# A state-space scan whose input is formed by TensorE from diagonals, in a two-layer block on one core

## The chip, the cores and the metric

The program runs on one core of a Trainium2 chip. The core has five engines that run beside each other and wait for one another through semaphores: TensorE (PE in the profile; its weight loads are listed apart as PEld), VectorE (DVE), ScalarE (ACT), GpSimd (POOL) and SyncE (SP), which here only issues DMAs. TensorE writes to PSUM, eight banks of 128 partitions by 512 fp32 values; the other tiles lie in SBUF. GpSimd reads and writes SBUF alone. The metric is the device time of one execution in microseconds (us), lower is better. Three runs of the kernel before took 4177.97, 4184.37 and 4188.32 us.

## The reference, cut to what matters

The input x has 8 sequences (batches) of 512 tokens with 256 channels, in fp32. A first layer adds a Mamba block and an FFN with weights and activations rounded to four bits; a second layer adds block-sparse attention and a two-layer local transformer. The change is nearly all in the first layer:

```
xn = layernorm(x)
x_in, z = split(xn @ W_in.T)              # 512 channels each
u = silu(causal_conv4(x_in) + conv_b)
d_raw, B, C = split(u @ W_xproj.T)        # 16, 16, 16 columns
delta = softplus(d_raw @ W_dt.T + b_dt);  A = -exp(A_log)
for each token t:                         # h: 512 channels x 16 states
    h = exp(delta[t] * A) * h + (delta[t] * u[t]) * B[t]
    y[t] = sum over states of h * C[t]
out = ((y + D_param * u) * silu(z)) @ W_out.T
x1 = x + out + fp4_ffn(xn)
```

fp4_ffn rounds xn, the hidden activations and its three weight matrices in blocks of 16 values. The second layer then works on x1.

## The kernel before, in words

The first stage (pools of `s0`, the kernel's lines 143 to 378) handles one batch after another. Channels lie on partitions, in NC = 4 chunks of 128, and the 512 tokens run along the free axis. Four generators make up a batch. `head(b)` loads x, normalises it, transposes it (xt), forms u with a matmul and four VectorE operations per chunk, forms delta, and du = delta * u on GpSimd (line 272); it writes B and C to HBM (`bc_d`, line 252). `ffn(b)` does the four-bit FFN. `scan(b)` (lines 322 to 369) runs over two halves of two chunks, and in each half over the NS = 16 states. For one chunk and one state, called a unit here (64 units per batch, 512 in all), it does:

```
act.activation(da, delta[:, c, :], AF.Exp, scale=a_neg[:, c, n : n + 1])   # L338, into PSUM
dve.tensor_tensor(hh, du[:, c, :], bc[:, 0, :], ALU.mult)                  # L340
dve.tensor_tensor_scan(hh, da, hh, 0.0, ALU.mult, ALU.add)                 # L341
pool.tensor_tensor(hh, hh, bc[:, 1, :], ALU.mult)                          # L342
pe.matmul(ys[i], ident, hh, start=(n == 0), stop=(n == NS - 1))            # L343
```

bc holds one row of B and one of C, spread over all partitions by a DMA (line 330, SP's queue). The sum over states is a matmul with the identity that accumulates in a PSUM bank. After a half, z = silu(...) is formed by channels (line 349), D_param * u is added on VectorE (line 355) and the gate multiplied on GpSimd (line 358). At the end `ps_o` (line 364) projects out and the sum goes to HBM as x1.

Before the first head, ten blocks of weights are rounded to four bits and transposed: eight for w_gate and w_up (lines 177 to 194) and two for w_down (lines 209 to 213). `beside` interleaves generators in program order: scan(b) with the chain of ffn(b) and head(b+1), 34 steps against 24. That order gives priorities; the planner of the tile framework simulates the program and writes each engine's instruction order by priority and by what is ready in its simulation. On the chip each engine then runs its list strictly in that order, and waits at the first instruction whose inputs are not there. A tile's `bufs` says how many buffers rotate under its tag: `da` has two PSUM banks, `mm` four, the two sums `y0` and `y1` one each; `h` has four SBUF buffers, `bc` three.

The second stage (pools of `s1`, from line 381) first loads its weights, builds two rotary tables on VectorE and writes them to HBM (lines 431 to 444), all on SP's queue, then loads x1 of batch 0 (line 390, called by `proj(0)`), and runs attention and the transformer over the batches. Its tiles may use the memory of the first stage only when the first stage's pools have been released.

## Time and profile before

| | |
|---|---|
| median of three runs | 4184.37 us |
| the profiled execution | 4182.33 us, of which the profile's span is 4180.5 us |
| granted TensorE clock, mean over the span | 0.883 |
| first stage: first scan instruction, last output matmul ends | 111.9 us, about 1808 us |
| second stage: first matmul of `ps_qk` | 1850.5 us |
| busy share of the span: PE, DVE, ACT, POOL | 83%, 69%, 41%, 35% |

The profile has one row per group of equal instructions, with total busy time, the mean duration of one, and the idle time of the engine ahead of them with what ended it. A matmul's duration includes some 0.17 us in which the result leaves the array while the next one already runs, so durations of matmuls overlap, and what a stream of them costs is read from the distance between starts. An fp32 matmul appears as two instructions of the same shape, each with its own weight load; a transpose of 128 x 128 appears as one.

### The profile page before, as it was taken

How to read it: one execution, taken by the hardware profiler on the slowest of the kernel's cores; microseconds unless marked ns; L12 is line 12 of the kernel's file. 1: busy time of each engine (PE TensorE's matmuls, PEld its weight loads, DVE VectorE, ACT ScalarE, POOL GpSimd, SP SyncE). 2: the span in 40 equal slices, each digit the busy share in tenths (PEclk: the TensorE clock that was granted, in tenths of full speed). 3: DMA queues.
4: the chain of work that ended last, by engine and by line, in shares of the span. 5: the costliest groups of instructions: out<-in, count | busy, mean ns of one | idle time of the engine just before them, and what ended most of it. 6: DMA issues, size and time to landing. Idle time of an engine off the chain costs nothing.

```text
span 4180.5 us, 40473 instructions
## 1 busy us (share of the span) xinstructions
PE 3488.5 (83%) x13932; PEld 1700.7 (41%) x13932; DVE 2892.1 (69%) x4825; ACT 1721.5 (41%) x3411; POOL 1456.9 (35%) x1059
## 2 busy tenths in 40 slices
PE   3677777777777777759999999999989999999998
PEld 1233333333333333324454544554554544445445
DVE  6899999999999999955545545654555455456454
ACT  2454545555454545414423333343243244234333
POOL 2666665657575757521111120111021011101211
PEclk9777787787887888879999999999999999999999
DMA  2333233333332323330111010010011101110100
GB/s 63 76 81 91 77 90 80 87 81 86 78 88 80 87 76 90 80 120 26 42 37 37 31 57 26 26 52 30 27 52 42 37 26 42 36 47 26 47 27 6
DMA packets 121606, 239.27 MB, mean 57 GB/s; under 512 B 10025, under 2 KB 41769, under 8 KB 121401
## 3 DMA queue, kind: packets, MB, share of 16 engines
q1 hardware_dynamic: 118464, 230.32, 19.7%
q10 hardware_dynamic: 2936, 6.36, 0.4%
q8 instruction: 111, 1.82, 0.2%
q14 instruction: 95, 0.77, 0.1%
HBM read 226.69 MB, written 9.96 MB: 57 GB/s over the span
## 4 chain that ended last, share of the span: by engine, by line
PE 46%; DVE 10%; issue 3%; ACT 2%; POOL 2%; DMA 1%; SPq 0%; POOLq 0%; DVEq 0%; ACTq 0%
PE ps_qkv L683 8%; PE ps_g L853 5%; PE ps_a L853 4%; PE ps_qk L514 3%; PE ps_wo L815 3%; PE ps_y L888 2%; PE ps_w L871 2%; PE ps_st L609 2%; PE lo L787 2%; PE ps_ls L735 2%; PE pt_qk L674 2%; DVE pr L764 2%; DVE nm L745 1%; PE pt L773 1%; DVE hh L341 1%
## 5 line engine op out<-in xcount | busy, mean ns | idle before, releaser
L343 PE MATMUL y<-hh,ident 128*128 128x512 f32 x1024 | 692.3, 789 | 407.5 <-POOL hh L342 406.1
L342 POOL TENSOR_TENSOR hh<-hh,bc 128x512 f32<-128x512 f32 x512 | 754.0, 1482 | 553.9 <-issue 130.3
L341 DVE TENSOR_TENSOR_SCAN hh<-da,hh 128x512 f32<-128x512 f32 x512 | 609.4, 1205 | 1.9 <-ACT da L338 1.2
L340 DVE TENSOR_TENSOR hh<-du,bc 128x512 f32<-128x512 f32 x512 | 575.6, 1145 | 32.8 <-PE y L343 23.8
L338 ACT ACTIVATE da<-delta,a_neg 128x512 f32<-128x512 f32 x512 | 349.3, 689 | 488.4 <-DVE hh L341 486.6
L343 PEld LDWEIGHTS y<-hh,ident 128*128 128x128 f32 x1024 | 204.1, 231 | 813.1 <-POOL hh L342 739.9
L702 POOL TENSOR_TENSOR r<-r,r 128x512 f32<-128x512 f32 x128 | 162.8, 1272 | 385.4 <-DVE r L700 385.4
L751 ACT ACTIVATE pr<-ps_ls,nm 128x256 f32<-128x256 f32 (+1 forms) x512 | 221.7, 446 | 176.7 <-DVE nm L745 176.6
L860 DVE SCALAR_TENSOR_TENSOR ht<-ps_a,b,gl 128x512 f32<-128x512 f32 x96 | 72.0, 750 | 264.1 <-PE ps_a L853 261.2
L463 POOL MEMSET sa<- 128x1 f32 x16 | 1.6, 98 | 725.4 <-DVE sa L819 386.2
L698 DVE TENSOR_TENSOR r<-ps_qkv,tab 128x512 f32<-128x512 f32 x128 | 87.9, 686 | 220.6 <-ACT sq L697 220.6
L853 PE MATMUL ps_g<-hn,wf 128*128 128x512 f32 (+1 forms) x384 | 212.1, 671 | 24.9 <-issue 24.3
L859 ACT ACTIVATE gl<-ps_g,b 128x512 f32<-128x512 f32 x96 | 65.9, 686 | 392.3 <-PE ps_g L853 392.3
L697 ACT ACTIVATE sq<-ps_qkv 128x512 f32<-128x512 f32 x128 | 76.6, 598 | 293.2 <-PE ps_qkv L683 293.2
L853 PE MATMUL ps_a<-hn,wf 128*128 128x512 f32 (+1 forms) x384 | 197.1, 634 | 0.0
L613 ACT ACTIVATE pt_e<-ps_st 128x512 f32<-128x512 f32 (+1 forms) x384 | 172.8, 536 | 15.2 <-PE ps_st L607 14.6
L745 DVE TENSOR_REDUCE nm<-ps_ls 128x2 f32<-128x512 f32 (+1 forms) x256 | 147.5, 618 | 44.7 <-PE ps_ls L735 43.8
L683 PE MATMUL ps_qkv<-wqkv,s 128*128 128x512 f32 x384 | 174.7, 604 | 0.0
L683 PE MATMUL ps_qkv<-wqkv,sf 128*128 128x512 f32 x384 | 173.4, 601 | 0.0
L764 DVE TENSOR_SCALAR pr<-pr,lrs 128x256 f32<-128x256 f32 (+1 forms) x512 | 148.7, 332 | 4.8
L338 ACT ACT_TABLE_LOAD x115 | 147.5, 1283 | 5.8 <-DVE hh L341 3.8
L735 PE MATMUL ps_ls<-lkt,lqt 64*128 64x256 f32 (+1 forms) x1024 | 140.0, 396 | 0.0
(212 smaller groups left out, 6450.8 us busy)
## 6 DMA issues: line engine op xcount, KB each, us to landing
bc<-bc_d SPq DMA_DIRECT2D x256, 512.0 KB, 4.9
wqkv<-in_wqkv SPq DMA_DIRECT2D x16, 1536.0 KB, 6.4
wf<-in_wf SPq DMA_DIRECT2D x16, 1364.0 KB, 5.9
wf<-in_wf SPq DMA_DIRECT2D x16, 768.0 KB, 4.8
tab<-tab SPq DMA_DIRECT2D x18, 512.0 KB, 4.3
wo<-in_wo SPq DMA_DIRECT2D x16, 512.0 KB, 3.9
x<-in_x SPq DMA_DIRECT2D x8, 512.0 KB, 5.4
x<-xs ACTq DMA_DIRECT2D x8, 512.0 KB, 5.8
```

Source lines behind the costliest of these rows:

```text
L338: act.activation(da, delta[:, c, :], AF.Exp, scale=a_neg[:, c, n : n + 1])
L340: dve.tensor_tensor(hh, du[:, c, :], bc[:, 0, :], ALU.mult)
L341: dve.tensor_tensor_scan(hh, da, hh, 0.0, ALU.mult, ALU.add)
L342: pool.tensor_tensor(hh, hh, bc[:, 1, :], ALU.mult)
L343: pe.matmul(ys[i], ident, hh, start=(n == 0), stop=(n == NS - 1))
L613: act.activation(pt[:, :n], banks[g][:, :n], AF.Exp)
L683: pe.matmul(ps, shifted(s, k, t * P, P), wqkv[:, k, i * IN : (i + 1) * IN], start=(k == 0), stop=(k == KC - 1),)
L735: pe.matmul(banks[r][:, i * nk : (i + 1) * nk], qt[LD * r : LD * (r + 1), 2 * p + i, w * P : (w + 1) * P], kt[LD * r : LD * (r + 1), 2 * p ...
L745: dve.tensor_reduce(nm, banks[r][:, : 2 * nk].rearrange("p (g n) -> p g n", g=2), AX.X, ALU.max, negate=True)
L751: act.activation(pr[:, at], banks[r][:, at], AF.Exp, bias=nm[:, i : i + 1], accum_out=rs[:, i : i + 1],)
L764: dve.tensor_scalar(pr[:, at], pr[:, at], rs[:, i : i + 1], None, ALU.mult)
L853: pe.matmul(dst[:m], wf1[:, k, off + c * P : off + c * P + m], hn[:, k, :], start=(k == 0), stop=(k == KC - 1),)
```

## The change

The change has five parts. (1) The product of du and B is taken from VectorE. `head` transposes du to tokens (`dut`) and B to tokens (`bt`). For each state, VectorE builds once per batch four diagonal matrices of B (`dg`, 128 x 512), and for each unit TensorE forms bu = dut^T x diag(B) with four fp32 matmuls of 128 columns, in PSUM (three banks, tag `bu`). The scan reads bu from PSUM, and the decay `da` now lies in SBUF. (2) The sum over states is done by `add`: four transposes of 128 x 128 that accumulate in PSUM, so that y comes out by tokens. D_param * u is scaled on ScalarE and enters the same sum. (3) The gate z is formed by tokens, multiplied on VectorE with y, transposed back on TensorE (`ps_zt`, `zt`) and projected out. (4) The rounding of the FFN's weights becomes a generator that runs beside scan(0), and the rotary tables are made behind it, with fewer and larger VectorE operations. (5) Buffers: `mm` has three banks for four; the spread DMA carries C alone; `xn`, `xd`, `xq` and `xs` lose buffers or go; the ffn yields more often; the second stage's pools may take memory tile by tile (`reuse_waits="tile"`), x1 of batch 0 is loaded first there, and the first `fetch` comes after `proj(0)`.

```diff
-        pmm = s0.enter_context(tc.tile_pool(name="pmm0", bufs=4, space=PSUM))
-        pda = s0.enter_context(tc.tile_pool(name="pda0", bufs=2, space=PSUM))
+        pmm = s0.enter_context(tc.tile_pool(name="pmm0", bufs=3, space=PSUM))
+        pbu = s0.enter_context(tc.tile_pool(name="pbu0", bufs=3, space=PSUM))
...
-        for name, dst in (("w_gate", w_g), ("w_up", w_u)):
...
-        for r in range(D // P):
...
+        def fp4_weights():
+            for name, dst in (("w_gate", w_g), ("w_up", w_u)):
+                src = a[name].rearrange("(j p) d -> p j d", p=FB)
+                for j in range(0, FI // FB, 2):
+                    raw = q.tile([P, FI], FP, tag="q_src", name="q_src")[:FB, : 2 * D]
+                    act.dma_start(raw.rearrange("p (j d) -> p j d", j=2), src[:, j : j + 2, :])
+                    fp4(raw, raw, FB, 2 * D, q, sm)
...
+                    yield
...
+        tab_d = [dram.tile([P, 4, NT, LD], FP, tag=f"tab_{l}", bufs=1, name=f"tab_{l}") for l in range(DEPTH)]
+
+        def rotary_tables():
+
+            for l in range(DEPTH):
+                tab = one.tile([P, NT, DI], FP, tag="z", name="tab")[:, :2, :].rearrange("p (i t) (u d) -> p (i t u) d", t=1, d=LD)
+                tab = tab.rearrange("p (i t) d -> p i t d", t=NT)
+                sp.dma_start(tab, a["rotary"])
+                for i, name in ((0, "q_scale"), (2, "k_scale")):
+                    qs = sm.tile([P, LD], FP, tag="qs", bufs=2, name="qs")
+                    sp.dma_start(qs, a[name][l].unsqueeze(0).to_broadcast([P, LD]))
+                    if i == 0:
+                        dve.tensor_scalar(qs, qs, 8.0, None, ALU.mult)
...
+                    for at, cols, sc in ((i, lo, lo), (i, hi, hi), (i + 1, lo, hi), (i + 1, hi, lo)):
+                        dve.tensor_tensor(tab[:, at, :, cols], tab[:, at, :, cols], by(sc), ALU.mult)
+                sp.dma_start(tab_d[l], tab)
+                yield
...
-            xn = w1.tile([P, NT, D], FP, tag="xn", name="xn")
+            xn = one.tile([P, NT, D], FP, tag="xn", name="xn")
...
-            xd = w1.tile([DR + 2 * NS, L], FP, tag="xd", name="xd")
+            xd = w1.tile([DR + 2 * NS, L], FP, tag="xd", bufs=1, name="xd")
             act.copy(xd, ps[: DR + 2 * NS, :])
-            bc_d = dram.tile([2 * NS, L], FP, tag="bc_d", name="bc_d")
-            sp.dma_start(bc_d, xd[DR:, :])
+            c_d = dram.tile([NS, L], FP, tag="c_d", name="c_d")
+            sp.dma_start(c_d, xd[DR + NS :, :])
+
+            nx = DR + 2 * NS
+            ps = pmm.tile([P, L], FP, tag="mm", name="ps_bt")
+            for t in range(NT):
+                pe.transpose(ps[:, t * nx : (t + 1) * nx], xd[:, t * P : (t + 1) * P], ident[:nx, :nx])
+            bt = w1.tile([P, NT, NS], FP, tag="bt", name="bt")
...
-            du = w1.tile([P, NC, L], FP, tag="du", name="du")
+            dut = w1.tile([P, NT, DI], FP, tag="dut", name="dut")
...
-                pool.tensor_tensor(du[:, c, :], delta[:, c, :], u[:, c, :], ALU.mult)
-                yield
-            made[b] = x, xn, xt, u, bc_d, delta, du
+
+                pool.tensor_tensor(e, delta[:, c, :], u[:, c, :], ALU.mult)
+                yield
+                ps = pmm.tile([P, L], FP, tag="mm", name="ps_du")
+                for t in range(NT):
+                    pe.transpose(ps[:, t * P : (t + 1) * P], e[:, t * P : (t + 1) * P], ident)
+                evac(dut[:, :, c * P : (c + 1) * P], ps.rearrange("p (t d) -> p t d", d=P))
+            yield
+            made[b] = x, xn, xt, u, c_d, bt, delta, dut
...
+                    yield
...
-                ys = [py.tile([P, L], FP, tag=f"y{i}", name=f"y{i}") for i in range(2)]
+                ys = [py.tile([P, NT, P], FP, tag=f"y{i}", name=f"y{i}") for i in range(2)]
+
+                def add(y, src, first, last):
+
+                    for t in range(NT):
+                        pe.matmul(
+                            y[:, t, :], src[:, t * P : (t + 1) * P], ident, is_transpose=True,
+                            start=(first and t == 0), stop=(last and t == NT - 1), skip_group_check=True,
+                        )
+
+                for i in range(2):
+                    c = c0 + i
+                    ud = rot.tile([P, L], FP, tag="h", bufs=5, name="ud")
+                    act.activation(ud, u[:, c, :], AF.Copy, scale=d_par[:, c : c + 1])
+                    add(ys[i], ud, True, False)
                 for n in range(NS):
-                    bc = rot.tile([P, 2, L], FP, tag="bc", name="bc")
-                    sp.dma_start(
-                        bc,
-                        bc_d.rearrange("(t n) l -> n t l", n=NS)[n].unsqueeze(0).to_broadcast([P, 2, L]),
-                    )
+                    cb = rot.tile([P, L], FP, tag="cb", name="cb")
+                    sp.dma_start(cb, c_d[n].unsqueeze(0).to_broadcast([P, L]))
+                    if c0 == 0:
+                        dg[n] = one.tile([P, NT, P], FP, tag=f"dg{n}", name=f"dg{n}")
+                        dve.tensor_tensor(
+                            dg[n], ident.unsqueeze(1).to_broadcast([P, NT, P]),
+                            bt[:, :, n : n + 1].to_broadcast([P, NT, P]), ALU.mult,
+                        )
                     for i in range(2):
                         c = c0 + i
-
-                        da = pda.tile([P, L], FP, tag="da", name="da")
+                        bu = pbu.tile([P, L], FP, tag="bu", name="bu")
+                        for t in range(NT):
+                            pe.matmul(
+                                bu[:, t * P : (t + 1) * P], dut[:, t, c * P : (c + 1) * P], dg[n][:, t, :],
+                                start=True, stop=True,
+                            )
+                        da = rot.tile([P, L], FP, tag="da", name="da")
                         act.activation(da, delta[:, c, :], AF.Exp, scale=a_neg[:, c, n : n + 1])
-                        hh = rot.tile([P, L], FP, tag="h", bufs=4, name="hh")
-                        dve.tensor_tensor(hh, du[:, c, :], bc[:, 0, :], ALU.mult)
-                        dve.tensor_tensor_scan(hh, da, hh, 0.0, ALU.mult, ALU.add)
-                        pool.tensor_tensor(hh, hh, bc[:, 1, :], ALU.mult)
-                        pe.matmul(ys[i], ident, hh, start=(n == 0), stop=(n == NS - 1))
+                        hh = rot.tile([P, L], FP, tag="h", bufs=5, name="hh")
+                        dve.tensor_tensor_scan(hh, da, bu, 0.0, ALU.mult, ALU.add)
+                        pool.tensor_tensor(hh, hh, cb, ALU.mult)
+                        add(ys[i], hh, False, n == NS - 1)
                     yield
-                for i in range(2):
-                    c = c0 + i
+                for t in range(NT if c0 == 0 else 0):
                     ps = pmm.tile([P, L], FP, tag="mm", name="ps_z")
                     for k in range(KC):
                         pe.matmul(
-                            ps, w_in[:, k, DI + c * P : DI + (c + 1) * P], xt[:, k, :],
+                            ps, xt[:, k, t * P : (t + 1) * P], w_in[:, k, DI:],
                             start=(k == 0), stop=(k == KC - 1),
                         )
-                    z = rot.tile([P, L], FP, tag="t1", name="z")
-                    act.activation(z, ps, AF.Silu)
-                    dve.scalar_tensor_tensor(
-                        u[:, c, :], u[:, c, :], d_par[:, c : c + 1], ys[i], ALU.mult, ALU.add
-                    )
-                    pool.tensor_tensor(u[:, c, :], u[:, c, :], z, ALU.mult)
-                yield
-            xs = sums.pop(b)
...
+                    act.activation(z[:, t, :], ps, AF.Silu)
+                for i in range(2):
+                    zc = z[:, :, (c0 + i) * P : (c0 + i + 1) * P]
+                    dve.tensor_tensor(zc, zc, ys[i], ALU.mult)
+                yield
             for t in range(NT):
+                ps = pmm.tile([P, L], FP, tag="mm", name="ps_zt")
+                for c in range(NC):
+                    pe.transpose(ps[:, c * P : (c + 1) * P], z[:, t, c * P : (c + 1) * P], ident)
+                zt = rot.tile([P, NC, P], FP, tag="zt", bufs=1, name="zt")
+                evac(zt, ps.rearrange("p (c n) -> p c n", n=P))
                 ps = pmm.tile([P, L], FP, tag="mm", name="ps_o")
                 for c in range(NC):
-                    pe.matmul(
-                        ps[:, :D], u[:, c, t * P : (t + 1) * P], w_o[:, c, :],
-                        start=(c == 0), stop=(c == NC - 1),
-                    )
-                dve.tensor_tensor(xs[:, t, :], xs[:, t, :], ps[:, :D], ALU.add)
-            act.dma_start(x1_d[b], xs)
-
-        sums = {}
+                    pe.matmul(ps[:, :D], zt[:, c, :], w_o[:, c, :], start=(c == 0), stop=(c == NC - 1))
+                dve.tensor_tensor(x[:, t, :], x[:, t, :], ps[:, :D], ALU.add)
+            act.dma_start(x1_d[b], x)
...
-            beside(scan(b), chain(*rest), 34, 24)
+            if b == 0:
+                rest = [fp4_weights(), *rest, rotary_tables()]
+            beside(scan(b), chain(*rest), 34, 37 if b else 49)
...
-        w0 = s1.enter_context(tc.tile_pool(name="w1", bufs=1))
...
+        w0 = s1.enter_context(tc.tile_pool(name="w1", bufs=1, reuse_waits="tile"))
...
+        x1_first = load_x1(0)
...
-            x1 = x1s[b] = load_x1(b)
+            x1 = x1s[b] = load_x1(b) if b else x1_first
...
-        fetch(0, 0, "wqkv", "tab", "wo", "wf1", "wf2")
         tc.keep_in_program_order(act.preload_act_table_set("natural_log_exp_and_others"))
         alone(proj(0))
+        fetch(0, 0, "wqkv", "tab", "wo", "wf1", "wf2")
```

## The prediction

> **What bounds the kernel now.** I read the page first, then its groups, then busy time by stretches, then who waited for whom, and last the order of time around short matmuls.
>
> The page says PE 83% and DVE 69%, but these are means over two stages:
>
> ```profile
> PE   3677777777777777759999999999989999999998
> DVE  6899999999999999955545545654555455456454
> PEclk9777787787887888879999999999999999999999
> ```
>
> After the first slice of 104.5 us come sixteen with VectorE at 80 to 90% or more and TensorE at 60 to 70% on a clock of 0.7 to 0.8; then they change places. The change lies in the first stage, so VectorE's rows count there:
>
> ```profile
> L343 PE MATMUL y<-hh,ident 128*128 128x512 f32 x1024 | 692.3, 789 | 407.5 <-POOL hh L342 406.1
> L342 POOL TENSOR_TENSOR hh<-hh,bc 128x512 f32<-128x512 f32 x512 | 754.0, 1482 | 553.9 <-issue 130.3
> L341 DVE TENSOR_TENSOR_SCAN hh<-da,hh 128x512 f32<-128x512 f32 x512 | 609.4, 1205 | 1.9 <-ACT da L338 1.2
> L340 DVE TENSOR_TENSOR hh<-du,bc 128x512 f32<-128x512 f32 x512 | 575.6, 1145 | 32.8 <-PE y L343 23.8
> L338 ACT ACTIVATE da<-delta,a_neg 128x512 f32<-128x512 f32 x512 | 349.3, 689 | 488.4 <-DVE hh L341 486.6
> ```
>
> The scan waits for nobody (1.9 us of idle time in 512), ACT waits for the scan, TensorE waits for GpSimd. By stretches (us, busy PE, PEld, DVE, ACT, POOL with counts, then the granted clock, the DMA share, GB/s):
>
> ```profile
> 400.00:1600.00 1200.00, 895.79 (x2010) 392.61 (x2010) 1112.72 (x1310) 630.63 (x820) 749.72 (x512) 0.79 0.33 83
> 1757.00:1803.00 46.00, 32.20 (x68) 11.21 (x67) 41.09 (x40) 18.01 (x23) 27.61 (x21) 0.96 0.38 90
> 1803.00:1850.50 47.50, 6.14 (x25) 4.36 (x25) 15.04 (x85) 1.92 (x4) 6.22 (x14) 0.61 0.68 226
> ```
>
> VectorE is busy 92.7% of the steady stretch: it is the bound. The third line is the passage between the stages, 47.5 us with every engine idle most of the time. TensorE's waits in the same 1200 us:
>
> ```profile
> PEld y L343 <- POOL hh L342: 506.8, 223, 5.7
> PE y L343 <- POOL hh L342: 275.5, 161, 4.1
> ```
>
> In order of time, the first scan instruction starts at 111.9 us, later batches follow every 210.5 and then 215.0 us, the eighth begins at 1612.6 and ends at 1803.9. One batch therefore holds 0.927 x 215 = 199 us of VectorE, and by the same division 134 us of GpSimd and 113 us of ACT.
>
> **Short matmuls.** The change replaces 512-column matmuls by 128-column ones, so their price decides. Durations include the tail; I take start to next start in the second stage, where the clock is full:
>
> ```profile
> 2057.23 0.82 PE L674 MATMUL pt_qk<-ident,r 128*128 128x128 f32 x6
> 2057.89 0.38 PE L728 MATMUL ps_ls<-mask,identb 128*128 128x256 bf16 x2
> 2058.20 0.72 PE L735 MATMUL ps_ls<-lkt,lqt 64*128 64x128 f32 x8
> 2058.84 0.87 PE L78 MATMUL ps_tr<-ident,xn 128*128 128x128 f32 x6
> 2064.63 1.88 PE L514 MATMUL ps_qk<-s,wq 128*128 128x512 f32 x4
> 2066.35 0.60 PE L728 MATMUL ps_ls<-mask,identb 128*128 128x512 bf16 x2
> ```
>
> Six transposes take 2057.89 - 2057.23 = 0.66 us, 0.11 each. Four 512-column fp32 instructions take 1.72 us, 0.43 each, 0.84 ns per column. L735 is nearest to the new matmul: 128 columns with a weight load of 128 columns before each, in two halves of the rows side by side; a half does four in 0.64 us, first load included, so 0.16 each, and 0.11 if only the columns counted.
>
> **The cost, per unit (one chunk, one state; 64 per batch).**
> - VectorE loses L340: 72.0 us per batch. It gains 16 `dg` products per batch; the nearest row is L340 itself, whose instructions last 0.62 us undisturbed and 1.145 in the mean, so 9.9 to 18.3 us; I take 18. It gains two evacuations each of `dut` and `zt` (the copies of 128x512 in these rows last 0.69): 2.8. The gate product replaces L355 (0.75), nothing. VectorE: 199 - 72 + 18 + 3 = 148 us.
> - TensorE. Before, at full clock, per batch, columns at 0.84 ns: y 128 x 0.43 = 55; `ps_in` and `ps_z` 32 x 0.43 = 14; `ps_xp` and `ps_dt` 16 x 0.43 = 7; `ps_g`, `ps_u` 64 x 0.295 = 19; `ps_d`, `ps_o` 80 x 0.215 = 17; 40 transposes 4.4. That is 116 us in a batch of 215. After: y goes; `add` is four transposes, 0.44 per unit, 28 us; bu is eight instructions. Low end 0.11, the columns alone; high end 0.11 + 0.19 (the weight load's own duration) = 0.30. L735 shows the load hidden after the first, so 0.115: 0.92 per unit, 59 us. 48 further transposes (ud, `dut`, `zt`): 5. Sum 116 - 55 + 28 + 59 + 5 = 153 us.
> - GpSimd loses L358 (four of 1.27) and some of the disturbance by L340 (L342 has 1.26 undisturbed, 1.48 mean): 134 falls to 115 to 129. ACT gains four ud copies (0.69), half of the evacuations (0.6 each) and `bt`: 113 to 118; writing `da` to SBUF instead of PSUM is unseen here; its row is 0.69, the SBUF-to-SBUF exponential of `head` 0.62, so I take no change, and 5 us per batch of either sign.
> - DMA: half the bytes of bc. Only 4.8 us of waits on it are in the whole run; nothing.
>
> So the bound moves to TensorE: 153 us at full clock against 148 on VectorE. Two terms stretch it. The clock: 0.79 now, in gaps; 0.96 in the stretch 1757 to 1803, with TensorE only 70% busy but evenly so, and 0.95 over the second stage. With little idle time left I take 0.95: 161 us. Waits: `add` still waits for GpSimd in order, and bu of later units queues behind it on TensorE's list, and the scans behind bu. Now these waits are 275.5 / 1200 x 215 = 49 us per batch. Three banks of bu (3.6 us of scans) stand between, so I take half, 25 us. A batch: 186 us, against 215. A check: with columns at 0.84 ns and row or column groups side by side, the second stage's rows sum to about 1790 us of its 2330, 0.77; 153 / 186 is 0.82.
>
> **The Trainium skill against this.** "TensorE: Matmul & The Clock Gate", Part 4, says that a transpose costs about 275 ns in a kernel and does not count as activity for the clock. The durations here agree (0.27), the pitch of 0.11 does not, and the clock holds through the transposes above. By the page's figure `add` would be 64 x 4 x 0.275 = 70 us instead of 28, the batch about 230 and the total about 4215 us. I go by the pitch.
>
> **Moved work.** The ten weight blocks leave the front. x lands at 13.9 us; its normalisation takes 6; from the first transpose of xn (71.3) to the first scan (111.9) are 40.6; with the new transposes and the first dg and bu I put the first scan at 63, 49 us earlier. Their cover is scan(0), where they cost VectorE ten passes of 3.0 to 3.8 us and copies, 36 us, and the tables 5: 148 + 41 = 189, at 92.7% busy 204. Ten loads move onto ACT's queue beside the exponentials, and eight table DMAs onto SP's, where cb of scan(1) queues behind a table that waits for z's buffer; a few us each, so 210 for batch 0: no change. If batch 0's cover fails, at most those 41 us come back.
> Between the stages, x1 is loaded at 1840.2 behind the tables' round trips; weights arrive from 1808. Without them x1 comes with the weights, and the first `ps_qk` starts about 20 us after the scan's end instead of 46.6: 27 us, between 12 (only the last table's wait) and 45 (memory freed early). What is late next is the weights' own load, 5 us. The deferred fetch has 45 us until its first use.
>
> **Sum** on the profiled execution (4182.3, 2 us under the median): front -49, batch 0 0, six batches 6 x -29 = -174, last batch 191 to 166 (no head beside it) -25, passage -27: -275. 4182 - 275 = 3907 us.
>
> **Rivals.**
> - *Engines overlap better.* No lasting waits for GpSimd; VectorE binds at 148 / 0.927 = 160 and TensorE at 161, batch 165. Seven times 21 less: 3760 us. For it: even supply in a scan-only stretch. Against: two engines this full with three banks between.
> - *TensorE waits as now.* The whole 49 us stay: 161 + 49 = 210; seven times 24 more: 4075 us. For it: GpSimd's long rounding products (1.7 us) and 4 us waits. At a clock of 0.79 it would be the same with 16 us of waits.
> - *Slower: bu's weight loads are not hidden.* At 0.30 per instruction bu is 154 us, TensorE 248, a batch 286, seven and three quarter times 100 more, about 4680 us. It decides from the point where 275 us are eaten: 275 x 0.95 over 7.6 x 512 instructions is 0.067 us more, a pitch of 0.18. L735 speaks against it, but with half the rows each.
> - *It does little:* gain and stalls cancel, a batch near 222, about 4182.
>
> **How the numbers follow.** My case 0.42 (3830 to 3990), better overlap 0.20, waits as now 0.20, slower 0.15, no change 0.03. A run of this kernel tells 0.3%, 12 us, from no change. Faster 0.82, same 0.03, slower 0.15. The range runs from 3750, the better overlap, to 4190; it leaves out the slower case and the tail below.
>
> **What the next profile would show.** If right: in the scan's steady stretch TensorE above 90% busy at a clock above 0.9, VectorE near 80%; the scan row idle for PE's bu; bu's starts 0.11 to 0.12 apart; first scan near 63 us; `ps_qk` near 1575. Wrong if bu's starts lie 0.18 or more apart, if the clock stays at 0.8, or if `add` waits 40 us or more per batch for GpSimd.

## The result

The changed kernel takes 4304.52 us (median of four runs, 4297.69 to 4305.67), the kernel before 4181.17 beside it (four runs, 4168.83 to 4188.32): a ratio of 1.0305, 95% interval 1.0279 to 1.0331. It is slower by 3%, where a gain of 6.6% was forecast, and above the upper end of the range, 4190. The profiled execution of the changed kernel took 4297.69 us, its span 4295.9.

Time by stages, from the starts of the first scan instruction of each batch in both traces. A "steady batch" is here and below the mean of batches 1 to 6; the last batch is counted to the start of its last scan instruction.

| stage | before, us | after, us | difference | forecast |
|---|---|---|---|---|
| start to first scan | 111.9 | 56.8 | -55 | -49 |
| batch 0 | 210.5 | 283.8 | +73 | 0 |
| a steady batch (six) | 215.0 | 233.7 | +18.7 (+112) | -29 (-174) |
| last batch | 186.4 | 209.2 | +23 | -25 |
| last scan to first `ps_qk` | 51.5 | 24.7 | -27 | -27 |
| from `ps_qk` to the end | 2330 | 2319 | -11 | 0 |

What was moved out of the front and the passage came out as forecast. Everything that has a scan in it went the other way.

The page of the changed kernel, busy tenths in 40 slices:

```profile
PE   5587877787877778778999999999999999999998
DVE  5766666657575766655564455555545655555454
PEclk7898989898999989898999999999999999999999
```

VectorE fell from 8 and 9 tenths to 5 to 7 in the scan's slices, as it should, but TensorE did not take its place: 7 and 8 tenths. No engine is full any more. The same over the six steady batches (us, then busy PE, PEld, DVE, ACT, POOL with counts, the granted clock, the DMA share, GB/s):

```profile
340.60:1742.70 1402.10, 1093.35 (x6310) 830.04 (x6311) 914.79 (x1163) 682.69 (x905) 709.35 (x528) 0.93 0.14 43
```

A batch holds 915 / 6 = 152 us of VectorE, where 148 were forecast, and 1093 / 6 = 182 us of busy TensorE at a clock of 0.93, where 161 (153 at full clock, stretched by 0.95) were. The groups of the page that answer to those of before:

```profile
L405 POOL TENSOR_TENSOR hh<-hh,cb 128x512 f32<-128x512 f32 x512 | 690.6, 1355 | 798.3 <-DVE hh L404 712.0
L404 DVE TENSOR_TENSOR_SCAN hh<-da,bu 128x512 f32<-128x512 f32 x512 | 613.7, 1211 | 275.1 <-PE bu L397 250.5
L374 PE MATMUL y<-ident,hh 128*128 128x128 f32 x2048 | 354.3, 299 | 325.7 <-POOL hh L405 322.3
L397 PE MATMUL bu<-dg,dut 128*128 128x128 f32 x4096 | 577.8, 289 | 5.4 <-DVE hh L404 5.3
```

The scan, which waited 1.9 us before, now waits 250.5 us for bu in the whole run; bu itself waits for almost nothing, but the `add` (L374) that stands between two bu on TensorE's list waits 322.3 us for GpSimd. Who waits for whom in the six steady batches (us, times, longest):

```profile
DVE hh L404 <- PE bu L397: 183.1, 155, 3.7
PE y L374 <- POOL hh L405: 239.8, 273, 3.6
DVE h L346 <- PE ps_u L341: 76.1, 36, 3.0
...
PE ps_du L310 <- POOL e L306: 47.7, 24, 4.4
```

The last two lines are of the other work: the feed-forward's product on VectorE waits for TensorE, and the new transposes `ps_du` wait for GpSimd's `e`. They turned out to be the ones to follow. The price of the short matmuls is not the cause, as a stretch of the timeline shows (start, us, engine, line, operation, count):

```profile
1252.33 1.28 PE L397 MATMUL bu<-dg,dut 128*128 128x128 f32 x10
1253.54 0.45 PE L283 MATMUL ps_bt<-ident,xd 48*128 48x48 f32 x4
...
1260.46 0.66 PE L374 MATMUL y<-ident,hh 128*128 128x128 f32 x4 [1.29 <-POOL hh L405]
1260.95 0.61 PE L397 MATMUL bu<-dg,dut 128*128 128x128 f32 x4
```

Ten bu in 1253.54 - 1252.33 = 1.21 us, 0.12 each; over all of them the median from start to start is 0.112, the forecast's 0.115. The last two lines show the order: bu starts when the `add` ahead of it has waited its 1.29 us for GpSimd.

### The profile page after: what moved, and what is told of

Read it like the earlier page. It is cut to its first block, busy times and chain, and to the rows that moved or that the text cites. A ratio compares the mean times of both kernels' runs of the same rounds, so it can differ in the third digit from the quotient of the medians.

```text
span 4295.9 us, 51035 instructions
## 1 busy us (share of the span) xinstructions
PE 3660.6 (85%) x19452; PEld 2249.7 (52%) x19468; DVE 2503.9 (58%) x4441; ACT 1727.3 (40%) x3446; POOL 1321.0 (31%) x1027
## 4 chain that ended last, share of the span: by engine, by line
PE 56%; DVE 19%; POOL 12%; issue 8%; ACT 3%; DMA 1%; DVEq 0%; POOLq 0%; ACTq 0%; SPq 0%
PE ps_qkv L732 7%; POOL hh L405 7%; DVE hh L404 6%; PE ps_g L902 4%; PE ps_a L902 4%; PE bu L397 3%; PE y L374 3%; PE ps_qk L563 3%; PE ps_wo L864 3%; PE ps_y L937 2%; PE ps_w L920 2%; PE ps_st L658 2%; PE lo L836 2%; PE ps_ls L784 2%; PE pt_qk L723 2%
## 5 line engine op out<-in xcount | busy, mean ns | idle before, releaser
L405 POOL TENSOR_TENSOR hh<-hh,cb 128x512 f32<-128x512 f32 x512 | 690.6, 1355 | 798.3 <-DVE hh L404 712.0
L404 DVE TENSOR_TENSOR_SCAN hh<-da,bu 128x512 f32<-128x512 f32 x512 | 613.7, 1211 | 275.1 <-PE bu L397 250.5
L374 PE MATMUL y<-ident,hh 128*128 128x128 f32 x2048 | 354.3, 299 | 325.7 <-POOL hh L405 322.3
L397 PE MATMUL bu<-dg,dut 128*128 128x128 f32 x4096 | 577.8, 289 | 5.4 <-DVE hh L404 5.3
L397 PEld LDWEIGHTS bu<-dg,dut 128*128 128x128 f32 x4096 | 539.8, 205 | 46.4 <-issue 14.4
L402 ACT ACTIVATE da<-delta,a_neg 128x512 f32<-128x512 f32 x512 | 362.1, 720 | 420.0 <-DVE hh L404 331.4
L374 PEld LDWEIGHTS y<-ident,hh 128*128 128x128 f32 x2048 | 232.3, 148 | 482.4 <-POOL hh L405 448.7
L747 DVE TENSOR_TENSOR r<-ps_qkv,tab 128x512 f32<-128x512 f32 x128 | 87.8, 686 | 221.1 <-ACT sq L746 221.1
L662 ACT ACTIVATE pt_e<-ps_st 128x512 f32<-128x512 f32 (+1 forms) x384 | 172.8, 536 | 15.2 <-PE ps_st L656 14.5
L402 ACT ACT_TABLE_LOAD x111 | 142.4, 1283 | 67.8 <-DVE hh L404 56.8
```

The costliest lines, as they stand in the source:

```text
L374: pe.matmul(y[:, t, :], src[:, t * P : (t + 1) * P], ident, is_transpose=True, start=(first and t == 0), stop=(last and t == NT - 1), skip ...
L397: pe.matmul(bu[:, t * P : (t + 1) * P], dut[:, t, c * P : (c + 1) * P], dg[n][:, t, :], start=True, stop=True,)
L404: dve.tensor_tensor_scan(hh, da, bu, 0.0, ALU.mult, ALU.add)
L405: pool.tensor_tensor(hh, hh, cb, ALU.mult)
L662: act.activation(pt[:, :n], banks[g][:, :n], AF.Exp)
```

## The experiments

Two things can make a batch long with no engine full. One is the scan's own ring: bu, scan, multiply, add, and the next bu behind that add. The other is the strand beside it: a chain of steps, here called links (head, delta steps, end of the scan before, feed-forward, next head), that follow one another through four engines. The runs came in this order. Each was timed beside the kernel before (medians of 4168 to 4180 us); four probes, which leave work out, ran once each.

### First round: the places that the profile shows

**The add two units later.** The `add` of a unit is kept back until two more units' bu are on TensorE's list:

```
-                        add(ys[i], hh, False, n == NS - 1)
+                        late.append((ys[i], hh, False, n == NS - 1))
+                        if len(late) > 2:
+                            add(*late.pop(0))
...
+                while late:
+                    add(*late.pop(0))
```

> Edit: the four accumulating transposes of a unit are issued two units later, so that TensorE builds bu two units ahead of the scan; nothing else changes. Theory A (the slow steady batch is a ring: bu, scan, GpSimd's multiply, add, and the next bu queued behind that add): VectorE's waits for bu, 30 us a batch, fall to 10 or less, a batch from 233.7 to about 205 us, the whole to about 4080 us. Rival B (the stop between the two halves and the tail of the batch before cost it, not the order of bu and add): a batch within 5 us of 233.7, the whole within 40 us of 4305. Rival C (TensorE, busy 78% and slowed by its clock, is full in all but name): no change either, with TensorE's waits merely moved from add to bu.

Measured: 4213.64 us, ratio to before 1.0088 (1.0054 to 1.0122); a steady batch 221.7. TensorE's order has bu 1.89 units ahead of the `add` in the mean, 1.09 before the edit. VectorE's wait in its six steady batches:

```profile
DVE hh L405 <- PE bu L398: 96.8, 77, 4.5
```

96.8 instead of 183.1 us, 14 a batch saved of which 12 arrive. So the ring is real, but worth 12 us, not the 28 that theory A had, and not rival B's nothing.

**z early.** The four tiles of z are issued inside the first half's states:

```
+                    if c0 == 0 and n in (3, 6, 9, 12):
+                        gate((3, 6, 9, 12).index(n))
                     yield
-                for t in range(NT if c0 == 0 else 0):
-                    ps = pmm.tile([P, L], FP, tag="mm", name="ps_z")
...
-                    act.activation(z[:, t, :], ps, AF.Silu)
```

In the changed kernel's batch 0 the scan stands at the half boundary; y's buffer waits for the gate product, that for z, and z for `ps_z`, which runs only after the feed-forward's tiles that stand before it (first TensorE, then VectorE):

```profile
228.50 7.13 PE L411 MATMUL ps_z<-w_in,xt 128*128 128x512 f32 x16
```

```profile
236.30 1.28 DVE L418 TENSOR_TENSOR z<-z,y 128x512 f32<-128x512 f32 x2 [7.27 <-ACT z L415]
237.88 2.33 DVE L404 TENSOR_TENSOR_SCAN hh<-da,bu 128x512 f32<-128x512 f32 x2 [0.30 <-PE y L374]
```

> Edit: the four token tiles of z (ps_z and its silu) are issued inside the first half's states, after states 3, 6, 9 and 12, instead of after state 15. Theory A (at the half boundary the scan stands because y has one buffer, which waits for z, which waits for the mm ring): the stop of batch 0 (some 72 us without a scan) falls to under 15, that of a steady batch (25.3 us for four units where 10 to 15 are usual) by about 10; the whole falls by 60 + 7 x 10 = 130 to about 4175 us. Rival (batch 0 is long because the serial weights chain holds mm and the engines, wherever z stands): the stop only moves, batch 0 stays above 260 us, and the whole falls by less than 70 us.

Measured: 4323.1 us, 1.0349 (1.0312 to 1.0386): slower still. Batch 0 takes 275.4 us, its four units at the half boundary still 59.6 (82.6 in the changed kernel), a steady batch 239.1. Theory A fell: the stop got 23 us shorter, but batch 0 only 8, and a steady batch 5 longer.

**Both.** The two diffs above together.

> Edit: both of the two before, the add two units later and z inside the first half. If the two losses are separate, the gains add up: with both theories right a steady batch of about 195 us, batch 0 of about 215, the whole about 3950 us, faster than the kernel before. If one hides the other, the sum of the two gains is not reached; if neither counts, about 4300 us.

Measured: 4274.89 us, 1.0237 (1.0205 to 1.0269); steady batch 232.3, batch 0 272.4. z early takes back nearly all of the 12 us that the later add gives.

**Weights at the front again.**

```
+        alone(fp4_weights())
         for _ in head(0):
...
-                rest = [fp4_weights(), *rest, rotary_tables()]
-            beside(scan(b), chain(*rest), 34, 37 if b else 49)
+                rest = [*rest, rotary_tables()]
+            beside(scan(b), chain(*rest), 34, 37 if b else 39)
```

> Edit: the feed-forward weights are quantized ahead of the first head again, as in the kernel before, and not beside scan 0; the rotary tables stay beside it. Theory (moving them costs as much in batch 0 as it saves ahead of it): the first scan starts about 105 us in (56.8 in the changed kernel), batch 0 falls from 283.8 to about 235 us, and the whole stays within 20 us of 4305. Rival (batch 0's stop comes from z and y alone): the first scan starts 50 us later, batch 0 stays above 265 us and the whole rises by 30 us or more.

Measured: 4306.27 us, 1.0308 (1.0273 to 1.0343), first scan at 109.2 us, batch 0 227.4, steady batch 233.7. Batch 0 loses 56 us and the front gains 52. So the move of the weights is worth nothing, whatever its cover looked like, and it has no part in the steady batches.

### Second round: banks, or a strand that sets the batch

**Banks dealt anew**, on top of the later add: `pmm0` with four buffers, `pbu0` with two.

> Edit: on top of the add two units later (4213.6 us, steady batch 221.7, batch 0 276.8) the PSUM banks are dealt anew: four for mm (three) and two for bu (three). Theory A (what is left of the loss is the mm ring: it lost a bank, and the other strands, z among them, queue for it): a steady batch falls by 8 us or more, batch 0 below 260, the whole to about 4120 us. Rival B (the ring of mm is not short; the steps wait for one another through four engines whatever the banks): a batch within 3 us of 221.7, the whole 4200 to 4230. Rival C (bu needs its third bank): a batch 5 us or more longer, VectorE's waits for bu up again, the whole above 4255 us.

Measured: 4212.11 us, 1.0074 (1.005 to 1.0098); steady batch 221.1, as rival B expected. VectorE's waits for bu in the six steady batches stay where the later add had left them, 96.9 us and 96.8, so no loss of bu's hides a gain of mm's: in this order neither ring is short.

**z from bu's ring**, on top of the later add and z early: `ps_z` takes `pbu.tile(..., tag="bu")`.

> Edit: the add two units later, z inside the first half as in the run that issued z early, and ps_z takes a bank of bu's ring and not of mm's. Theory A (z early did not help because ps_z still queued in the mm ring behind the feed-forward's tiles): z is ready before the half boundary, the 81 us without a scan in batch 0 fall below 25, the four units at the boundary of a steady batch from 25.8 to about 12, a steady batch from 221.7 to about 209, batch 0 to about 220, the whole to about 4070 us. Rival B (the chain of the other strands sets the batch, and the scan waits for it at whatever place): the stop at the boundary is gone but comes back at another place, a steady batch stays within 4 us of 221.7 and batch 0 above 260, the whole above 4180 us.

Measured: 4208.49 us, 1.0075 (1.0051 to 1.01); steady batch 223.3, batch 0 262.7. The stop at the boundary is gone, as the scan instructions between 160 and 245 us show, first in the changed kernel, then here (count, duration min/median/max in ns, first and last start):

```profile
L404 DVE TENSOR_TENSOR_SCAN hh<-da,bu x5: 1153/1195/1221, 160.5 to 240.1; 128x512 f32<-128x512 f32 x5
```

```profile
L416 DVE TENSOR_TENSOR_SCAN hh<-da,bu x26: 1159/1207/1222, 165.7 to 241.6; 128x512 f32<-128x512 f32 x26
```

26 scans instead of 5 in the same 85 us, and yet batch 0 is only 14 us shorter than with the later add alone, and the steady batch not at all: from the start of batch 0's last four units to the next batch's first scan it is now 69.8 us. What comes late there is the next head's `dut`, on VectorE's list of this run (start, us):

```profile
314.86 0.69 DVE L50 COPY dut<-ps_du 128x512 f32<-128x512 f32 x1 [5.01 <-PE ps_du L310]
...
318.94 1.22 DVE L416 TENSOR_TENSOR_SCAN hh<-da,bu 128x512 f32<-128x512 f32 x1 [2.18 <-PE bu L409]
```

The scan runs ahead and then waits for the strand. This is what rival B expected: the longest waits of the scan are where it meets the strand, and taking one away moves them to another place.

**The kernel before with three mm banks** (`pmm0` `bufs=3`).

> Edit: the kernel before with three mm banks in the first stage and not four (one bank of PSUM left unused), nothing else. Theory A (the bank that the change takes from mm costs time by itself): a steady batch rises from 215.0 to 223 us or more, the whole to 4245 us or more. Rival B (the fourth bank was not needed): a batch within 2 us of 215, the whole 4165 to 4200 us.

Measured: 4215.75 us, 1.0089 (1.0058 to 1.012); steady batch 220.8. This lies between the two: the bank was worth 6 us a batch in the old order. In the new one, with the later add, it was worth nothing.

**The end of a scan beside the next**, on top of the later add: a generator `tail(b - 1)` with one `yield` per token tile heads the strands of scan b, and `zt` takes tag `t1`.

> Edit: the add two units later, and the end of a scan (transposes of z, the product with w_o, the sum into x) is issued beside the next scan, in four steps ahead of its feed-forward strand, and its zt takes one of the three t1 buffers and not one buffer of its own. Theory A (the scan's first sixteen units are slow, 69 us where 36 are usual, because the tail's steps wait for one another through one zt while the scan stands behind them): these units fall to about 55 us, a steady batch from 221.7 to about 208, the whole to about 4110 us. Rival B (building dg, 18 us of VectorE, and the end of head cost these units): they stay within 4 us of 69, the whole within 25 us of 4213.6.

Measured: 4276.71 us, 1.0233 (1.0206 to 1.026); steady batch 232.1, the first sixteen units 71 us. It is 10 us a batch worse, which neither theory had: the first units stay, as with rival B, and the feed-forward, which these steps now precede in the strand, takes longer, 128 us in the fourth batch against 116.

### Third round: the strand by itself

Read the strand in the traces, not the scan. With the first `e` of the delta steps, the last `dut` (`du` before), the first `xqt` and the last sum with `ps_d` as marks, a round falls into four pieces (us, mean of batches 1 to 6; the last two columns are runs told of below):

| piece | before | after | half the states, before | half, after |
|---|---|---|---|---|
| four delta steps | 41.2 | 62.2 | 36.4 | 58.1 |
| to the feed-forward (end of the scan before) | 10.9 | 14.1 | -4.1 | 15.2 |
| feed-forward | 128.9 | 126.6 | 130.2 | 110.2 |
| next head, to its delta steps | 34.0 | 30.8 | 19.8 | 18.3 |
| round | 215.0 | 233.8 | 182.3 | 201.7 |

Marks that come once in each batch always add up to the batch, whatever limits it, so the sums prove nothing; the runs below test whether the strand sets the length. What the table shows is where the 18.8 us of growth lie along the strand: 21.0 + 3.2 - 2.3 - 3.2, more than all of it in the delta steps. The rows of one head, before and then after (count, duration min/median/max in ns, first and last start; the last line says how long TensorE waited for GpSimd ahead of `ps_du`: us, times, longest):

```profile
L264 ACT ACTIVATE e<-ps_dt,b_dt x4: 665/666/676, 716.4 to 735.6; 128x512 f32<-128x512 f32 x4
...
L272 POOL TENSOR_TENSOR du<-delta,u x4: 1333/1670/1725, 730.0 to 755.9; 128x512 f32<-128x512 f32 x4
```

```profile
L297 ACT ACTIVATE e<-ps_dt,b_dt x4: 673/687/687, 787.4 to 835.1; 128x512 f32<-128x512 f32 x4
...
L52 ACT COPY dut<-ps_du x2: 585/585/585, 816.1 to 848.8; 128x512 f32<-128x512 f32 x2
...
PE ps_du L310 <- POOL e L306: 8.4, 4, 4.3
```

Before, the four `e` start within 19.2 us, since nothing holds `ps_dt` of the next tile. After, they take 47.7: TensorE's list has `ps_dt` of a tile behind `ps_du` of the tile before, and that one waits for three GpSimd steps. While it waits, 8.4 us in this head and 47.7 / 6 = 8.0 us a batch, bu and `add` stand behind it too. Its busy time, 16 transposes at a pitch of 0.11, would be 1.8 us.

**ps_du one tile later**, on the changed kernel alone:

```
-                ps = pmm.tile([P, L], FP, tag="mm", name="ps_du")
...
-                evac(dut[:, :, c * P : (c + 1) * P], ps.rearrange("p (t d) -> p t d", d=P))
+                late.append((c, e))
+                while len(late) > (1 if c < NC - 1 else 0):
+                    to_tokens(*late.pop(0))
             yield
```

> Edit, on the changed kernel alone: the transposes ps_du of a channel tile are issued one tile later in head, after the next tile's ps_dt and its steps. In the changed kernel the four delta steps run one after the other, 63 us (ps_dt at -21.0, -5.8, 9.0 and 25.9 us from a scan's start, the last dut at 42.3), because each ps_dt stands in TensorE's order behind a ps_du that waits for GpSimd; in the kernel before they overlapped, 42 us. Theory S (a batch is as long as one round of the serial strand head, delta steps, end of the scan before, feed-forward; the change made that round 21 us longer here): the four steps take 45 us or less, a steady batch falls from 233.7 to about 216, the whole by about 130 to 4175 us. Rival O (a batch is bound by the scan's own ring of bu, scan, multiply and add, and the strand runs beside it): the four steps get shorter, a steady batch stays within 5 us of 233.7, the whole above 4260 us.

Measured: 4243.19 us, 1.0173 (1.0134 to 1.0212); steady batch 227.0.

```profile
L306 ACT ACTIVATE e<-ps_dt,b_dt x4: 673/686/687, 764.5 to 786.5; 128x512 f32<-128x512 f32 x4
...
PE ps_du L298 <- POOL e L315: 2.3, 4, 1.1
```

The four `e` start within 22.0 us, `ps_du` waits 2.3. The four steps take 39.0 us in the fourth batch, so their whole excess is gone; but only 6.7 of 18.7 us arrive, between theory S (about 18) and rival O (5 or less). The feed-forward of that batch takes 144 us where it took 127. `add` waits for GpSimd as before (246.7 us in the six steady batches, 239.8 without the edit).

**Half of the states.** `range(NS // 2)` in the scan, whose 18 steps are dealt against the same strand.

> Probe, leaves work out: the scan runs over 8 of the 16 states, so half of bu, scans, multiplies, adds and dg are gone, and the strands beside it are unchanged. Theory S (the strand's round is the batch): a steady batch falls by less than 45 us, from 233.7 to 190 or more, though half of the scan's instructions are gone (39 of VectorE's 152 us of scans, 9 of dg, 87 of 175 us of GpSimd's and TensorE's of a batch). Rival O (the scan's ring): it halves with the units, a batch of 125 to 150 us.

Measured, one run: 4013.45 us, steady batch 201.7. Over its six steady batches, but for the last 5 us:

```profile
296.10:1502.00 1205.90, 856.90 (x3997) 614.65 (x3997) 625.79 (x922) 461.54 (x638) 432.75 (x336) 0.82 0.09 29
```

VectorE is busy 52%, GpSimd 36%, and the batch is only 32 us shorter, as theory S expected. In the fourth batch the scan stands still for 46.5 us at its end and for 44.5 us between its 19th and 20th unit: here it is the scan that waits for the work beside it.

**No feed-forward.** `ffn(b)` left out of the strands.

> Probe, leaves work out: the feed-forward strand is gone (x is summed with the scan's part alone); weights, heads and scans are unchanged. Theory S: a steady batch falls by about 90 us or more, since the strand's round loses its 121 us of feed-forward, to 150 or less, where the scan's own units (at the 2.2 to 2.4 us each that undisturbed stretches show) set it. Rival O: the batch falls only by what the feed-forward takes of the engines that the scan waits for, 30 us of VectorE and 25 of TensorE, to 180 or more.

Measured, one run: 3945.96 us, steady batch 193.6. Here theory S falls, in its simple form: 40 us less, not 90, and rival O's 180 or more holds. The four delta steps of the fourth batch take 82 us, now that the head's 11 steps are dealt over the scan's 34. So the scan with the strand's longest piece left out is 194, and the strand with half of the scan is 202; together they are 234. Neither alone is the batch: as far as these two runs show, each is made longer by the other in the same lists.

**Three edits together**: `ps_du` later, `add` later, z from bu's ring.

> Edit, three together: ps_du one channel tile later, the add two units later, z inside the first half from a bank of bu's ring. Theory S: with the strand's round shortened the earlier two count in full, a steady batch of about 200 us, batch 0 of about 245, the whole about 4030 us, faster than the kernel before by 3% or more. If the three overlap, about 4100 us. Rival O: nothing over the add alone, 4200 us.

Measured: 4128.24 us, 0.9888 (0.9852 to 0.9924): faster than the kernel before; steady batch 215.0. The 18.7 us are gone to the tenth, but not the 34 that theory S had. The later add alone had given 12.0 and the later `ps_du` alone 6.7, which is 18.7; z's bank had given nothing on top of the add (223.3 against 221.7). So two changes of order on TensorE's list, with no instruction less, undo the growth of the steady batch, and the larger part is the place of `add`. That `add` kept the later `ps_du` from giving more is not so: on top of the later add and z's bank it gives 8.3 (223.3 to 215.0), though the delta steps get 19 us shorter (60.3 to 41.0). Where the rest goes is open.

### Fourth round: was VectorE ever the bound?

**The kernel before without the product with B**, VectorE's 72 us a batch, with nothing in its place:

```
-                        dve.tensor_tensor(hh, du[:, c, :], bc[:, 0, :], ALU.mult)
-                        dve.tensor_tensor_scan(hh, da, hh, 0.0, ALU.mult, ALU.add)
+                        dve.tensor_tensor_scan(hh, da, du[:, c, :], 0.0, ALU.mult, ALU.add)
```

> Probe on the kernel before, leaves work out: VectorE's product of du with B is gone (the scan reads du), 64 instructions of 1.13 us or 72 us of VectorE a batch; nothing takes its place. Theory V (the prediction's first step: VectorE bound the kernel before, busy 199 of 215 us): a steady batch falls by 50 us or more, from 215.0 to 165 or less, the whole to about 3800 us. Theory S (the strand beside the scan was as long already, so VectorE's relief frees little): a batch of 190 or more, the whole above 3990 us.

Measured, one run: 3891.4 us, steady batch 181.7. The outcome lies between the two theories: 33 of VectorE's 72 us arrive.

**The kernel before with half of the states.**

> Probe on the kernel before, leaves work out: 8 of the 16 states, as in the same probe on the changed kernel (201 us a batch). Theory S (the change made the strand beside the scan about 21 us longer): a steady batch of about 180 us. Rival (the strand is as long before and after, and the changed kernel's scan alone makes the difference): 195 us or more, or (VectorE was the bound) 130 or less.

Measured, one run: 3905.45 us, steady batch 182.3, as theory S expected. The two windows of six steady batches, without B and with half of the states:

```profile
282.40:1372.80 1090.40, 865.65 (x2159) 397.60 (x2158) 831.09 (x1019) 644.43 (x853) 717.79 (x553) 0.90 0.37 98
```

```profile
298.10:1391.90 1093.80, 767.06 (x1776) 370.48 (x1775) 764.09 (x1014) 465.14 (x616) 507.32 (x360) 0.76 0.20 52
```

Two very different cuts end at the same 182 us, with VectorE busy 76% and 70%. With half of the states the scan of the fourth batch stands still for 89.7 us at its end, between the last scan instruction of that batch and the first of the next (start, us):

```profile
756.61 1.16 DVE L341 TENSOR_TENSOR_SCAN hh<-da,hh 128x512 f32<-128x512 f32 x1
...
847.44 2.33 DVE L341 TENSOR_TENSOR_SCAN hh<-da,hh 128x512 f32<-128x512 f32 x2
```

So there the strand sets the batch: under VectorE's 199 us lay a strand of about 182. Without B the scan never stands for more than 11.1 us in that batch, so that the strand is the limit there too is likely, not shown. The strand has no fixed length: without B the feed-forward takes 108.5 us and the next head 31.4, with half of the states 130.2 and 19.8. With half of the states the same strand is 201.7 in the changed kernel. The difference, 19 us, is about what the batch grew; by the table the delta steps have 21.7 of it, and the two pieces after them, taken together, are about as long (126.1 and 125.4). The other half of the scan adds about as much before, 215.0 - 182.3 = 33 us, as after, 233.7 - 201.7 = 32 us, though VectorE has 47 us a batch less to do.

**Feed-forward and next head turn by turn**, on top of the three edits:

```
-            rest = [ffn(b)] + ([head(b + 1)] if b + 1 < NB else [])
+            rest = [abreast(ffn(b), head(b + 1))] if b + 1 < NB else [ffn(b)]
```

> Edit, on top of the three edits together (4128 us, steady batch 215.0): the feed-forward of a batch and the head of the next are issued turn by turn after the feed-forward's third step, not one after the other. Theory S (the batch is the strand's length, one link after another): the two overlap, a steady batch falls to about 190 us, the whole to about 3950. Rival Q (the cost is that links and scan wait in the same written queues, whichever strand the links are of): a batch within 6 us of 215 or longer, the whole above 4090 us.

Measured: 3993.8 us, 0.9581 (0.9553 to 0.961); steady batch 197.3.

**Token tiles of the feed-forward overlapped**, on top of the three edits:

```
+            yield from gated(0)
             for t in range(NT):
+                fp4(hs[t], hs[t], P, FI, q, sm)
+                yield
+                if t + 1 < NT:
+                    yield from gated(t + 1)
+                down(t)
                 yield
```

> Edit, on top of the three edits together (4128 us, steady batch 215.0): in the feed-forward, the gate products of the next token tile are issued between a tile's quantization and its down product. Theory S: each tile's 26 to 30 us loses the 6 to 8 us of its gate products from the strand, a steady batch falls by 15 us or more to 200 or less, the whole to about 4010. Rival Q: a batch within 6 us of 215, the whole above 4080 us.

Measured: 3974.47 us, 0.9539 (0.9512 to 0.9565); steady batch 195.8. The feed-forward takes 109.0 us a batch instead of 131.2, the batch 19 less. Both runs fit theory S and not rival Q, the first with 18 of the 25 us that theory S had: a new order of the strand's links, with the same instructions, is worth about as much per batch as the change had cost.

**The end of a scan overlapped too**, on top of the run before: transposes of token tile t + 1 ahead of the product of t.

> Edit, on top of the feed-forward's overlapped token tiles (3974 us, steady batch 195.8): at the end of a scan the transposes of the next token tile are issued ahead of a tile's product with w_o, and zt takes the three t1 buffers. Theory S: these four links take 14 us of the strand, about 8 with the overlap, a steady batch falls by 4 to 6 us to about 190, the whole to about 3935. Rival T (TensorE, busy 171 of the 196 us, and the scan's queues set it now): a batch within 2 us of 195.8, the whole 3960 to 3990.

Measured: 3957.91 us, 0.9482 (0.9467 to 0.9496); steady batch 195.3. In the steady batches this is what rival T expected; the whole lies just under its 3960. In the two profiled executions, 10.8 us apart (the medians 16.6), the six steady batches give 3.0 us, the passage to the second stage 3.3, and the front, batch 0, the last batch and the second stage about 1 each.

**All of it.**

> Edit, all together: the run with the feed-forward's token tiles and the end of a scan overlapped, and the feed-forward and the next head issued turn by turn. Theory S: the strand is no longer the longest, a steady batch of about 180 us (TensorE's 171 and its waits), the whole about 3870. Rival T (TensorE's written queue, full to nine tenths, pays for each link put into it): a batch of 190 or more, the whole 3930 or more.

Measured: 3924.53 us, 0.9396 (0.938 to 0.9412), the fastest kernel of the study, 6% under the kernel before; steady batch 191.4, on rival T's side of the line; the whole is 5 us under rival T's 3930, and far above theory S's 3870. Its six steady batches:

```profile
299.80:1448.40 1148.60, 1003.74 (x6307) 809.94 (x6307) 938.04 (x1154) 711.70 (x930) 725.47 (x529) 0.96 0.18 51
```

TensorE is busy 87%, VectorE 82%: here the engines themselves begin to count. Which waits make up the 191 - 167 = 24 us of a batch in which TensorE idles is open; from the last four units to the next batch's first scan it is still 34.6 us, where four units usually take 8 to 13.

## Why the prediction was wrong

**What bounds the kernel: half right, and the half that was missing decides.** VectorE was busy 92.7% and it did bind: without the product with B a batch falls by 33 us. But it falls by 33 and not by 72, and with half of the states, where the scan stands and waits for it, the strand beside the scan is 182 us long. The step "it is the bound" took the fullest engine for the only limit. The prediction had no term for the strand at all; its price for a batch was the fullest engine plus its waits. A busy 92.7% does not show what lies 33 us under it.

**The batch of 186 us: wrong by 48, and this is the step that failed.** Engines: VectorE's 148 measured 152; TensorE's 161 measured 182 by busy records, which count tails too (at the pitches above, bu and `add` take 57 and 28 us a batch, where 59 and 28 were forecast), with the clock at 0.93 for 0.95. None of it is the limit at 233.7. The cuts of the kernel before ended at 182, so the forecast's 186 would have needed a strand that grew by nothing. The change lengthened it, by 19 us with half of the states: "48 further transposes (ud, `dut`, `zt`): 5" priced `ps_du` by its busy time, 4 x 4 x 0.11, and did not ask what stands in front of it (GpSimd's `e`) and what stands behind it (the next `ps_dt`, bu and `add`). That something which waits in order holds up what is queued behind it was said of `add`, and not of this. Of the 48 us, 18.7 are growth: 12.0 come back with the order of `add`, 6.7 with that of `ps_du`. The other 29 are a gain that did not come. With both orders mended a batch is 215.0 as before, with 47 us of VectorE less; overlapping links of the strand then brought it to 197 and 196. So what held back the gain there was the strand. How the 32 us come about that the second half of the scan still adds in the changed kernel stays open. Not tried alone were the single buffers of `xn` and `xd`, the sum into x, and the finer steps of the feed-forward.

**Waits of `add`: wrong.** Half of 49 us was forecast, 239.8 / 6 = 40 us a batch measured, the very bound that the prediction named as a sign of its being wrong. The three banks of bu did not stand between: TensorE's order has bu only 1.09 units ahead. Setting that right is worth 12.0 us a batch alone.

**Batch 0: wrong by 73.** "No change" rested on VectorE's room. The ten weight blocks are links of the strand too, and cost there what they had cost at the front: 56 us out of batch 0 and 52 us into the front when they are moved back. The other 17 us are about those of every batch. "At most those 41 us come back" was wrong because it counted VectorE's passes and not the chain.

**Last batch: wrong by 48**, with the steady ones and for the same reason.

**Front and passage: right.** First scan at 56.8 (63 forecast), the passage 27 us shorter as forecast.

**Short matmuls: right.** Pitch 0.112 for bu (0.115 forecast), 0.109 at the least for `add` (0.11). The rival that ended slower had the right sign by the wrong mechanism; the loads of the weights are hidden. "TensorE waits as now" had the waits nearer, 49 us, and still 4075 us, since it also knew only engines.

**The rule that was weighed.** The 275 ns a transpose of the Trainium skill, "TensorE: Matmul & The Clock Gate", Part 4, is the duration in this trace too (0.27), and the pitch is 0.109 to 0.12. Its total of about 4215 us came nearer to 4304 than the forecast, by the wrong road: not the clock and not the price of a transpose was what was lost.

**Another page of the Trainium skill would have pointed at the cause.** "PSUM — Partial Sum Buffer", section "Engine vs sequencer instructions", says that the queues of ScalarE, VectorE and GpSimd are strictly first in, first out, and that matmuls start in program order. The 8.4 us that `ps_du` holds up TensorE in one head, with bu behind it, agree.

The sum: six steady batches 6 x 47.7 = 286, batch 0 73, last batch 48, front -6, second stage -11: 390 us, but for rounding the distance of 4298 from 3907.

## What to carry to other kernels

Beside a loop that fills one engine, look for the second limit: follow the work that runs beside it from link to link. That its links add up to the round proves nothing; the test is cheap: leave out half of the loop, and if the round hardly falls and the loop stands still for long, the strand sets it. A transpose that waits for another engine costs what is queued behind it on the engine's list, not its busy time; issue it later, behind work that does not need it.

## What the runs showed of the hardware

- An fp32 128x128 matmul with weights of its own each time keeps a pitch of 0.112 us in the stream, in the median of bu: the load, 205 ns each in the records, is hidden.
- The granted clock of the steady batches rose from 0.79 to 0.93 with about the same share of busy TensorE (74% and 78%), and was 0.82 at 71% with half of the states. Neither the count of short matmuls nor the share alone was tested.
- VectorE's product for dg, with both operands broadcast, takes 1156 ns in the mean for 128x512 in the six steady batches, as long as the product with B that it stands in for (1135), with a quarter as many of them.
- GpSimd's multiply is little faster when VectorE has a quarter less to do: 1355 ns in the mean of the run against 1482.
